# Attention heads in pairs of groups: shared transposes, and maxima found further ahead

## The chip, the cores and the metric

One core of a Trainium2 chip runs the whole program in one launch. The metric is the device time of one execution in microseconds, median of five runs. All arithmetic is in float32.

## What is computed

Two transformer-like blocks over an input of 8 batches, 512 tokens, 128 channels. The change lies in the attention of the first block:

```python
h = layernorm(x) * (1 + ca) + sa
Q, K, V = (lora_linear(h, ...).reshape(8, 512, 16, 8) for each)      # 16 heads of 8 channels
energy = einsum('nqhd,nkhd->nhqk', Q, K) / sqrt(8)
out = einsum('nhqk,nkhd->nqhd', softmax(energy), V).reshape(8, 512, 128)
x = x + ga * lora_linear(out, Wo, ...)
```

Behind it come a mixture of experts (top 2 of 8, and a shared one), and a second block with a state-space scan and another mixture of experts, whose last layer uses the weight `fut`.

## The kernel before

**Groups.** The 128 channels of a batch lie on 128 partitions, which form four strips of 32 rows. Each strip holds four heads of 8 channels. A *group* is one head out of each strip, so a batch has four groups and all batches have 32, g = 0 to 31; `m = g % 4` is the head's place in its strip. `split(g)` (on GpSimd) multiplies queries and keys by a mask that leaves only head m of each strip, as `qt` and `kt`, and sets one spare row of `kt` to 1. When the spare row of `qt` holds minus the largest score of a query, the product of `kt` and `qt` is already shifted for the softmax.

**Steps and slots.** A group takes four *steps* (one for each 128 keys or queries) and each step has two halves, each half two strips. A *slot* is one half step; the work runs through `slot(s)` for s below zero (a start-up) to 255 and a little beyond. Group g has its scores in slots 8g to 8g + 7, a batch has 32 slots. In one slot:

- `scores(t, half)` multiplies `kt` and `qt` of two strips (matmuls `ps`, line 535); `exps` takes the exponentials on ScalarE into tiles `es`.
- `maxima(u, 1 - half)` multiplies the other way round on the other two strips (matmuls `pm`, line 488), for a step u that is `LEAD` = 6 steps ahead, and VectorE reduces to the largest of each row, into a column of a pad `mpad`. There is one pad for each m.
- then whatever is registered for the slot in the dictionary `after`, in the order in which it was registered.

`after` holds, relative to the group: `split(g)` at 8g - 16; `max_done(g)` at 8g - 3, which transposes the pad (four matmuls `pmt`, line 523) and subtracts it from `qt` on VectorE; `weigh(g, qc)` at 8g + 9, 11, 12, 13, which multiplies `es` by the values (`av`, line 556, 16 matmuls into the four column strips of one bank) and copies the bank to `part` on ScalarE; and `normalise(g)` at 8g + 15, which transposes `part` (four matmuls `ppt`, line 574), takes reciprocals of the sums and multiplies on VectorE into `o`. The values stand in `vaug`, 32 columns for each head: 8 of values, one of ones, and the rest zero.

Relative to the batch b (slots 32b + ...): `load_stats` (VectorE) at -40 to -37, `load_root` (GpSimd) at -35, `load_batch` at -30 (normalised tokens `xh`, on GpSimd), -24 (transposes `ptn`) and +20 (adds a bias to x, GpSimd); `project_batch` at -18 and -17 (matmuls `pqk`, then `qf` and `kf` on ScalarE); `values` at +2; `channels_back` at 42 (`pot`), `out_proj` at 46 (`py`, added to x on VectorE; its weight `wo` comes from GpSimd), `out_stats` at 47 to 50. From 51 on come the tokens' normalisation, the router's transposes `ptf` and product `pl`, the choice of experts, the counts `pcount`, and eight indirect writes (scatters) on GpSimd. Every engine works strictly in the order of the program.

**Buffers.** PSUM has two pools here: four banks (`sc`) that `ps`, `av`, `pmt`, `ppt`, `py` and the like take in turn, and two pairs of banks (`mx`) that `pm` and `pqk` take in turn. A buffer is free again when the last reader of it is done.

**Constants.** `fut_sb`, the weight of the last layer, is zeroed on GpSimd at the very start and loaded by four of the early DMAs; its use is in `ff_weights`, near the end.

Of the kernel before, what the change touches and what calls it, by code (L numbers as in the profile page):

```python
# [23 lines left out]
HD = 8  # L24
# [44 lines left out]
def tile_adaln_two_blocks(  # L69
# [51 lines left out]
    l1w_sb = ct([P, 10, D], "l1w_sb")  # L121
    rb_sb = ct([P, NE], "rb_sb")
    fdt_sb = ct([P, 32], "fdt_sb")
    fut_sb = ct([P, NC4, D], "fut_sb")
    fdb_sb = ct([P, 1], "fdb_sb")

    def load_later():

        Q.dma_start(out=wrout_sb, in_=wrout)
        Q.dma_start(out=b2_sb[0:NE, :], in_=b2)  # L130
        c_bs2 = COLS["bs2"][0]
        Q.dma_start(out=b2_sb[NE : NE + 1, :], in_=pcols[:, c_bs2 : c_bs2 + 1].rearrange("p o -> o p"))
        Q.dma_start(out=ws1, in_=w1t[:, NE, :])
        Q.dma_start(out=ws2, in_=w2t[:, NE, :, :])
        Q.dma_start(out=win_sb, in_=win)
        Q.dma_start(out=ssm_sb, in_=ssm)
        Q.dma_start(out=l1w_sb, in_=l1w)
        Q.dma_start(out=rb_sb, in_=rb.partition_broadcast(P))
        Q.dma_start(out=fdt_sb, in_=fdt)

        for c in range(NC4):
            g = slice(32 * c, 32 * c + 32)
            Q.dma_start(out=fut_sb[g, c, :], in_=fut)
            Q.dma_start(out=fdb_sb[g, :], in_=fdb)

    def col(name, i=0, n=1):
# [30 lines left out]
    G.memset(fut_sb, 0.0)  # L177
    zeros = ct([P, P], "zeros")
    V.memset(zeros, 0.0)
    mpads = []  # L180
    for m in range(4):
        mp = ct([P, NC4, P], f"mpad{m}")
        G.memset(mp, 0.0)
        mpads.append(mp)
# [111 lines left out]
    with tc.tile_pool(name="at", bufs=2) as at, tc.tile_pool(name="sc", bufs=4, space=PSUM) as psc, tc.tile_pool(  # L296
# [5 lines left out]
        for i in range(2):  # L302
            va = ate.tile([P, NC4, 16, 32], FP, tag=f"vaug{i}", name=f"vaug{i}")
            G.memset(va, 0.0)
            G.memset(va[:, :, :, HD], 1.0)
            vaugs.append(va)

        def pair(name):
# [159 lines left out]

        def split(g):

            b, m = g // 4, g % 4
            sp = (m + 1) % 4
            qt = ate.tile([P, S], FP, tag="qt", name="qt", bufs=3)
            kt = ate.tile([P, S], FP, tag="kt", name="kt", bufs=3)
            (V if g == 0 else G).tensor_scalar(qt, batch[b]["q"], mask[:, m : m + 1], zero, ALU.mult, ALU.add)
            G.tensor_scalar(kt, batch[b]["k"], mask[:, m : m + 1], spare[:, sp : sp + 1], ALU.mult, ALU.add)
            group[g] = (qt, kt)

        def maxima(u, half):

            g, qc = u // 4, u % 4
            qt, kt = group[g]
            r0 = HD * ((g + 1) % 4)
            pm = pair("pm")
            for i in range(2):
                r = 32 * (2 * half + i)
                pin(
                    T.matmul(  # L488
                        pm[:, i, :],
                        lhsT=qt[r : r + 32, qc * P : (qc + 1) * P],  # L490
                        rhs=kt[r : r + 32, :],
                        start=True,
                        stop=True,
                    )
                )
            mp = mpads[g % 4][:, qc, :].rearrange("p (j r) -> p j r", r=32)
            return lambda: V.tensor_reduce(mp[:, 2 * half : 2 * half + 2, r0], pm, AX.X, ALU.max)

        def maxima_first(u):

            g, qc = u // 4, u % 4
            qt, kt = group[g]
            r0 = HD * ((g + 1) % 4)
# [9 lines left out]
            mp = mpads[g % 4][:, qc, :].rearrange("p (j r) -> p j r", r=32)  # L513
            V.tensor_reduce(mp[:, 0:2, r0], pm, AX.X, ALU.max)
            for j in (2, 3):
                V.tensor_reduce(mp[:, j : j + 1, r0], banks[j], AX.X, ALU.max)

        def max_done(g):

            qt, _ = group[g]  # L520
            pt = bank("pmt")
            for c in range(NC4):
                pin(T.transpose(pt[:, c, :], mpads[g % 4][:, c, :], ident))  # L523
# [24 lines left out]
        def weigh(g, qc):  # L548
# [4 lines left out]
            for kc in range(NC4):  # L553
                for j in range(4):
                    pin(
                        T.matmul(  # L556
                            ps[32 * j : 32 * j + 32, 0, :],
                            lhsT=vaugs[b % 2][:, kc, 4 * j + m, :],
                            rhs=es_of[4 * g + kc, j][:, q],
                            start=(kc == 0),  # L560
                            stop=(kc == NC4 - 1),
                        )
                    )
            if qc == 0:
                part_of[g] = at.tile([P, NC4, P], FP, tag="part", name="part")
            A.copy(part_of[g][:, qc, :], ps[:, 0, :])

        def normalise(g):
# [8 lines left out]
            p4 = pt.rearrange("p c (j r) -> p c j r", r=32)  # L577
            rd = stat.tile([P, NC4, 4], FP, tag="rd", name="rd")
            V.reciprocal(rd, p4[:, :, :, HD])
            o4 = batch[b]["o"].rearrange("p c (j m d) -> p c j m d", j=4, m=4)[:, :, :, m, :]  # L580
            V.tensor_tensor(o4, p4[:, :, :, 0:HD], rd.unsqueeze(3).to_broadcast([P, NC4, 4, HD]), ALU.mult)

        def channels_back(b):
            o = batch[b]["o"]
# [45 lines left out]
        for i, (src, dst) in enumerate(rows):  # L630
            at_slot(3 + i, lambda src=src, i=i: mod_rows(src, i))
            at_slot(8 + i, lambda dst=dst, i=i: mod_rows_in(dst, i))
        for b in range(B):
            for c in range(NC4):
                at_slot(32 * b - 40 + c, lambda b=b, c=c: load_stats(b, c))
            if b == 0:
                at_slot(-35, lambda: load_root(0, 0))
                at_slot(-32, lambda: load_root(0, 1))
            else:
                at_slot(32 * b - 35, lambda b=b: load_root(b))  # L640
            for i, s in enumerate((-30, 20, -24)):
                at_slot(32 * b + s, lambda b=b, i=i: load_batch(b, i))
            for i in range(2):
                at_slot(32 * b - 18 + i, lambda b=b, i=i: project_batch(b, i))
# [249 lines left out]
        for i in range(TABLE):  # L894
            at_slot(32 * PB[0] + (45, 47, 49, 59, 60, 62, 63)[i], lambda i=i: table(0, i))

        def slot(s):
            t, half_ = s // 2, s % 2
            u = t + LEAD
            if t < 0 <= u and half_ == 0:  # L900
                maxima_first(u)
# [270 lines left out]
        def pointwise():  # L1172
# [355 lines left out]
        def ff_weights(b):  # L1528
            f = ffn[b]
            f["up"] = ek.tile([P, NC4, D], FP, tag="futg", name="futg", bufs=3)  # L1530
            gate = mpads[b // 4][:, b % 4 : b % 4 + 1, :].to_broadcast([P, NC4, D])
            (V if b == last else G).tensor_tensor(f["up"], fut_sb, gate, ALU.mult)

        def ff_up(b):

# [272 lines left out]
```

## Time and profile before

| what | value |
|---|---|
| median of five runs | 1064.18 us (1061.27 to 1064.9) |
| profiled execution: its time, its span | 1061.22 us, 1059.5 us |
| mean granted TensorE clock | 0.976 |
| TensorE, weight loads, VectorE, ScalarE, GpSimd busy | 95%, 62%, 61%, 60%, 45% |
| attention's slots 0 to 255 | from 35.1 us to about 539 us |
| `pmt` and `ppt` transposes | 128 and 128 matmuls, 21.0 and 21.2 us busy |

PE is TensorE, DVE VectorE, ACT ScalarE, POOL GpSimd, SP the queue that issues most DMAs. A timeline line gives start, duration, engine, source line, operation, what it writes and reads, and the count of records; a float32 matmul leaves two records where its rows are 512 long and its operands 32 rows deep. What stands in square brackets is the idle time before it, and who ended it. In a group's line the two numbers after the first bar are busy microseconds and mean nanoseconds of one.

### The profile page before, as it was taken

To read this page: it belongs to the slowest core of one execution; us is meant where nothing else is said; L and a number is where in the kernel's file an instruction comes from. 1 tells how busy PE (TensorE), PEld (TensorE's weight loads), DVE (VectorE), ACT (ScalarE), POOL (GpSimd) and SP (SyncE) were. 2 spreads that over 40 slices of the span, in tenths; PEclk is the share of its full clock that TensorE was granted. 3 is DMA by queue.
4 is the path that set the end of the run, shared out by engine and by line. 5 is a ranking of instruction groups with operands and counts; after the bars stand their busy time and mean duration, and the time that the engine had idled before them with its cause. 6 is when DMAs were issued, how large, how long until landed. Compare 5 with 4: busy or idle time off the path is not lost.

```text
span 1059.5 us, 24424 instructions
## 1 busy us (share of the span) xinstructions
PE 1002.2 (95%) x9656; PEld 659.7 (62%) x9656; DVE 649.4 (61%) x1279; ACT 636.4 (60%) x1401; POOL 480.5 (45%) x756
## 2 busy tenths in 40 slices
PE   9999999999999999999989999949999988989897
PEld 7555555555555555555569999838787656556455
DVE  5967686777768777777621124115586648858663
ACT  1466676666767667676645666414587465686553
POOL 3313143554726546354373134355633348556652
PEclk9999999999999999999999999969899999999999
DMA  6199200000000000000227886611364024314051
GB/s 173 41 305 284 90 12 2 9 24 2 29 4 14 20 4 29 2 26 8 66 66 222 242 252 201 178 52 31 104 181 120 26 78 144 100 61 140 11 190 40
DMA packets 94914, 94.90 MB, mean 90 GB/s; under 512 B 7848, under 2 KB 72832, under 8 KB 94800
## 3 DMA queue, kind: packets, MB, share of 16 engines
q1 hardware_dynamic: 90528, 84.65, 26.7%
q0 software_dynamic: 4096, 8.40, 2.6%
q8 instruction: 76, 1.25, 0.5%
q14 instruction: 38, 0.31, 0.1%
q10 hardware_dynamic: 176, 0.30, 0.1%
HBM read 61.96 MB, written 31.36 MB: 88 GB/s over the span
## 4 chain that ended last, share of the span: by engine, by line
PE 79%; POOL 7%; DVE 6%; ACT 5%; issue 3%; DVEq 0%; POOLq 0%; ACTq 0%
PE ps L535 23%; PE av L556 12%; PE pyb L1048 10%; PE ph L1037 10%; PE pm L488 3%; PE r L1445 2%; PE pe L1457 2%; PE pmt L523 2%; POOL t L65 2%; PE ppt L574 2%; PE pqk L448 1%; DVE xc L65 1%; PE pyb L1007 1%; PE pw L1357 1%; PE pxt L962 1%
## 5 line engine op out<-in xcount | busy, mean ns | idle before, releaser
L65 DVE TENSOR_REDUCE mpad<-pm 128x2 f32<-128x1024 f32 (+1 forms) x262 | 310.4, 1194 | 110.2 <-PE pm L488 107.1
L65 ACT ACTIVATE es<-ps 128x512 f32<-128x512 f32 x512 | 275.6, 598 | 160.0 <-PE pm L488 135.8
L535 PE MATMUL ps<-qt,kt 32*128 32x512 f32 x1024 | 291.2, 630 | 0.7 <-DVE x L65 0.6
L488 PE MATMUL pm<-kt,qt 32*128 32x512 f32 x976 | 261.5, 636 | 0.0
L556 PEld LDWEIGHTS av<-es,vaug 128*32 128x32 f32 x4096 | 104.2, 109 | 94.1 <-ACT part L65 43.2
L556 PE MATMUL av<-es,vaug 128*32 128x128 f32 x4096 | 137.7, 276 | 0.0
L535 PEld LDWEIGHTS ps<-qt,kt 32*128 32x128 f32 x1024 | 93.9, 183 | 61.5 <-issue 30.8
L65 ACT ACTIVATE hid<-ph,bias 128x256 f32<-128x256 f32 x184 | 72.2, 477 | 52.1 <-PE ph L1037 50.2
L1048 PEld LDWEIGHTS pyb<-w2b,hid 128*128 128x128 f32 x736 | 89.8, 192 | 6.2 <-ACT hid L65 3.4
L790 POOL DMA_INDIRECT x_rows<-tok,ux x64 | 65.2, 1019 | 62.4 <-DMA x_rows<-tok,ux 55.9
L1048 PE MATMUL pyb<-w2b,hid 128*128 128x128 f32 x736 | 90.7, 276 | 2.6 <-ACT hid L65 2.6
L1037 PE MATMUL ph<-xt,w1b 128*128 128x256 f32 x368 | 90.0, 388 | 1.6 <-issue 1.6
L1068 POOL DMA_INDIRECT yg<-y_rows,yrows x64 | 65.0, 1016 | 37.2 <-PE pgt L1000 18.7
L488 PEld LDWEIGHTS pm<-kt,qt 32*128 32x128 f32 x976 | 73.1, 183 | 8.7 <-ACT kf L65 5.4
L1037 PEld LDWEIGHTS ph<-xt,w1b 128*128 128x128 f32 x368 | 67.8, 195 | 10.0 <-issue 2.3
L65 POOL TENSOR_SCALAR qt<-qf,mask,zero 128x512 f32<-128x512 f32 x31 | 23.9, 772 | 109.9 <-PE pm L488 93.0
L1457 PE MATMUL pe<-x,l1w_sb 128*128 128x512 f32 x128 | 67.6, 624 | 4.6 <-ACT ye L65 4.5
L65 DVE COPY xt<-pxt 128x256 f32<-128x256 f32 x46 | 19.2, 419 | 85.1 <-PE pxt L962 76.9
L1445 PEld LDWEIGHTS r<-l1w_sb,t 128*128 128x128 f32 x368 | 47.6, 196 | 27.0 <-POOL t L65 12.2
L65 ACT ACTIVATE ye<-pe,pc 128x512 f32<-128x512 f32 x64 | 42.9, 683 | 32.4 <-PE pe L1457 26.6
L1445 PE MATMUL r<-l1w_sb,t 128*128 128x128 f32 x368 | 50.4, 282 | 9.1 <-POOL t L65 7.4
L65 ACT ACTIVATE hid<-ph,pc 128x256 f32<-128x256 f32 x64 | 25.2, 479 | 35.7 <-remote 19.0
(304 smaller groups left out, 1552.3 us busy)
## 6 DMA issues: line engine op xcount, KB each, us to landing
x_rows<-zeros SPq DMA_DIRECT2D x16, 1024.0 KB
gb<-g_rows SPq DMA_DIRECT2D x32, 512.0 KB
w1b<-in_w1t SPq DMA_DIRECT2D x46, 256.0 KB
w2b<-in_w2t SPq DMA_DIRECT2D x46, 256.0 KB
xg<-x_rows SPq DMA_DIRECT2D x46, 128.0 KB
y_rows<-yb SPq DMA_DIRECT2D x46, 128.0 KB
x<-in_x SPq DMA_DIRECT2D x8, 256.0 KB
h_chan<-hf SPq DMA_DIRECT2D x8, 256.0 KB
```

The lines of the kernel that those rows point to most:

```text
L65: return lambda *args, **kwargs: self.pin(call(*args, **kwargs))
L488: T.matmul(pm[:, i, :], lhsT=qt[r : r + 32, qc * P : (qc + 1) * P], rhs=kt[r : r + 32, :], start=True, stop=True,)
L523: pin(T.transpose(pt[:, c, :], mpads[g % 4][:, c, :], ident))
L535: T.matmul(ps, lhsT=kt[r : r + 32, kc * P : (kc + 1) * P], rhs=qt[r : r + 32, :], start=True, stop=True)
L556: T.matmul(ps[32 * j : 32 * j + 32, 0, :], lhsT=vaugs[b % 2][:, kc, 4 * j + m, :], rhs=es_of[4 * g + kc, j][:, q], start=(kc == 0), stop=( ...
L574: pin(T.transpose(pt[:, c, :], part[:, c, :], ident))
L790: nc.gpsimd.indirect_dma_start(out=x_rows[h], out_offset=IndirectOffsetOnAxis(ap=chosen["ux", b][:, k, c : c + 1], axis=0), in_=half[h]["t ...
L1037: pin(T.matmul(ph[:, f, :], lhsT=it["w1"][:, f * P : (f + 1) * P], rhs=it["x"], start=True, stop=True))
L1048: T.matmul(py[:, c, :], lhsT=it["hid"][:, f, c * P : (c + 1) * P], rhs=it["w2"][:, f, :], start=(f == 0 and "shared" not in it), stop=(f = ...
L1068: nc.gpsimd.indirect_dma_start(out=gathered[b][:, k, c, :], out_offset=None, in_=y_rows[h], in_offset=IndirectOffsetOnAxis(ap=half[h]["yro ...
L1445: T.matmul(ffn[b]["r"][:, c, :], lhsT=x[:, c * P : (c + 1) * P], rhs=w, start=(start and c == 0), stop=stop, skip_group_check=True,)
L1457: pin(T.matmul(pe, lhsT=l1w_sb[:, 2 + e, :], rhs=x1s[b], start=True, stop=True))
```

## The change

Groups 2k and 2k + 1 become a pair. Both write their maxima into one pad, in different columns (the spare row moves from head m + 1 to m + 2 of the strip), so from group 6 on one set of transposes serves two groups: `max_done(g, 2)` at 8g - 3 for even g, with two updates of `qt`. Groups 0 to 5 keep a set each (`PAIRED` = 6). The values of odd heads stand 16 columns further right in `vaug`, so the results of a pair don't overlap: the even group's `weigh` copies to `part` on ScalarE as before, the odd group's adds to the same `part` on VectorE, and `normalise` serves both, at 8g + 23.

Maxima of both groups of a pair must be there before the first is used. They still begin six steps ahead; in each of the slots 13, 17, ... 41 (`TWICE`) a second half follows, so that they are ten steps ahead from slot 41 on, and end after slot 235 instead of 243. `split` moves to 8g - 24 with four buffers, and the loading of batch 1 comes two slots earlier, that of later batches eight slots earlier; `values` moves to -4. Two pads go, and `fut_sb` is zeroed (VectorE) and loaded in the second block.

```diff
-    for m in range(4):
+    for m in range(2):
         mp = ct([P, NC4, P], f"mpad{m}")
...
+    TWICE = range(13, 45, 4)
+    PAIRED = 6
...
-            A.copy(
-                vaugs[b % 2].rearrange("p c h r -> p (c h) r")[:, :, 0:HD],
-                flat(ps).rearrange("p (c d) -> p c d", d=HD),
-            )
+            for e in range(2):
+                A.copy(
+                    vaugs[b % 2].rearrange("p c (n e) r -> p (c n) e r", e=2)[:, :, e, 16 * e : 16 * e + HD],
+                    flat(ps).rearrange("p (n e d) -> p n e d", e=2, d=HD)[:, :, e, :],
+                )
...
-            sp = (m + 1) % 4
-            qt = ate.tile([P, S], FP, tag="qt", name="qt", bufs=3)
+            sp = (m + 2) % 4
+            qt = ate.tile([P, S], FP, tag="qt", name="qt", bufs=4)
...
-            mp = mpads[g % 4][:, qc, :].rearrange("p (j r) -> p j r", r=32)
+            mp = mpads[g // 2 % 2][:, qc, :].rearrange("p (j r) -> p j r", r=32)
...
-        def max_done(g):
+        def max_done(g, n):
             pt = bank("pmt")
             for c in range(NC4):
-                pin(T.transpose(pt[:, c, :], mpads[g % 4][:, c, :], ident))
-            V.scalar_tensor_tensor(qt, flat(pt), -1.0, qt, ALU.mult, ALU.add)
+                pin(T.transpose(pt[:, c, :], mpads[g // 2 % 2][:, c, :], ident))
+            for k in range(n):
+                qt, _ = group[g + k]
+                V.scalar_tensor_tensor(qt, flat(pt), -1.0, qt, ALU.mult, ALU.add)
...
+            if g % 2:
+                part = part_of[g - 1][:, qc, :]
+                V.tensor_tensor(part, part, ps[:, 0, :], ALU.add)
+                return
...
-            at_slot(8 * g - 16, lambda g=g: split(g))
-            at_slot(8 * g - 3, lambda g=g: max_done(g))
+            at_slot(8 * g - 24 if g > 4 else (-16, -8, 0, 8, 14)[g], lambda g=g: split(g))
+            if g < PAIRED:
+                at_slot(8 * g - 3, lambda g=g: max_done(g, 1))
+            if g % 2 == 0:
+                if g >= PAIRED:
+                    at_slot(8 * g - 3, lambda g=g: max_done(g, 2))
+                at_slot(8 * g + 23, lambda g=g: normalise(g))
...
-            at_slot(8 * g + 15, lambda g=g: normalise(g))
...
+            early_by = (0, 2)[b] if b < 2 else 8
+            t = 32 * b - early_by
...
-            at_slot(32 * b + 2, lambda b=b: values(b))
+            at_slot(32 * b - 4 if b else 2, lambda b=b: values(b))
...
+        to_find = iter([(u, h) for u in range(LEAD, STEPS) for h in (1, 0)])
...
-            reduce = maxima(u, 1 - half_) if 0 <= t and u < STEPS else None
+            reduce = [maxima(*u) for _, u in zip(range((s >= 0) + (s in TWICE)), to_find)]
             exps(t, found)
-            if reduce is not None:
-                reduce()
+            for do in reduce:
+                do()
...
+            fut_sb = k1["fut"] = lt([P, NC4, D], "fut_sb")
+            V.memset(fut_sb, 0.0)
+            for c in range(NC4):
+                Q.dma_start(out=fut_sb[32 * c : 32 * c + 32, c, :], in_=fut)
```

More of the change, by code (lines that the diff above doesn't have):

```diff
@@ L123, in tile_adaln_two_blocks @@
     fdt_sb = ct([P, 32], "fdt_sb")
-    fut_sb = ct([P, NC4, D], "fut_sb")
     fdb_sb = ct([P, 1], "fdb_sb")
@@ L142, in load_later @@
             g = slice(32 * c, 32 * c + 32)
-            Q.dma_start(out=fut_sb[g, c, :], in_=fut)
             Q.dma_start(out=fdb_sb[g, :], in_=fdb)
@@ L176, in tile_adaln_two_blocks @@
     V.memset(zero, 0.0)
-    G.memset(fut_sb, 0.0)
     zeros = ct([P, P], "zeros")
@@ L304, in tile_adaln_two_blocks @@
             G.memset(va, 0.0)
-            G.memset(va[:, :, :, HD], 1.0)
+            for e in range(2):
+                G.memset(va.rearrange("p c (n e) r -> p c n e r", e=2)[:, :, :, e, 16 * e + HD], 1.0)
             vaugs.append(va)
@@ L463, in values @@
                 )
-            A.copy(
-                vaugs[b % 2].rearrange("p c h r -> p (c h) r")[:, :, 0:HD],
-                flat(ps).rearrange("p (c d) -> p c d", d=HD),
-            )
+            for e in range(2):
+                A.copy(
+                    vaugs[b % 2].rearrange("p c (n e) r -> p (c n) e r", e=2)[:, :, e, 16 * e : 16 * e + HD],
+                    flat(ps).rearrange("p (n e d) -> p n e d", e=2, d=HD)[:, :, e, :],
+                )
         def split(g):
             b, m = g // 4, g % 4
-            sp = (m + 1) % 4
-            qt = ate.tile([P, S], FP, tag="qt", name="qt", bufs=3)
-            kt = ate.tile([P, S], FP, tag="kt", name="kt", bufs=3)
+            sp = (m + 2) % 4
+            qt = ate.tile([P, S], FP, tag="qt", name="qt", bufs=4)
+            kt = ate.tile([P, S], FP, tag="kt", name="kt", bufs=4)
             (V if g == 0 else G).tensor_scalar(qt, batch[b]["q"], mask[:, m : m + 1], zero, ALU.mult, ALU.add)
@@ L482, in maxima @@
             qt, kt = group[g]
-            r0 = HD * ((g + 1) % 4)
+            r0 = HD * ((g + 2) % 4)
             pm = pair("pm")
@@ L502, in maxima_first @@
             qt, kt = group[g]
-            r0 = HD * ((g + 1) % 4)
+            r0 = HD * ((g + 2) % 4)
             pm = pair("pm")
@@ L512, in maxima_first @@
                 )
-            mp = mpads[g % 4][:, qc, :].rearrange("p (j r) -> p j r", r=32)
+            mp = mpads[g // 2 % 2][:, qc, :].rearrange("p (j r) -> p j r", r=32)
             V.tensor_reduce(mp[:, 0:2, r0], pm, AX.X, ALU.max)
@@ L516, in maxima_first @@
                 V.tensor_reduce(mp[:, j : j + 1, r0], banks[j], AX.X, ALU.max)
-        def max_done(g):
-            qt, _ = group[g]
+        def max_done(g, n):
             pt = bank("pmt")
             for c in range(NC4):
-                pin(T.transpose(pt[:, c, :], mpads[g % 4][:, c, :], ident))
-            V.scalar_tensor_tensor(qt, flat(pt), -1.0, qt, ALU.mult, ALU.add)
+                pin(T.transpose(pt[:, c, :], mpads[g // 2 % 2][:, c, :], ident))
+            for k in range(n):
+                qt, _ = group[g + k]
+                V.scalar_tensor_tensor(qt, flat(pt), -1.0, qt, ALU.mult, ALU.add)
         def scores(t, half):
@@ L576, in normalise @@
                 batch[b]["o"] = at.tile([P, NC4, D], FP, tag="o", name="o", bufs=1)
-            p4 = pt.rearrange("p c (j r) -> p c j r", r=32)
-            rd = stat.tile([P, NC4, 4], FP, tag="rd", name="rd")
+            p4 = pt.rearrange("p c (j e r) -> p (c j) e r", j=4, e=2)
+            rd = stat.tile([P, NC4 * 4, 2], FP, tag="rd", name="rd")
             V.reciprocal(rd, p4[:, :, :, HD])
-            o4 = batch[b]["o"].rearrange("p c (j m d) -> p c j m d", j=4, m=4)[:, :, :, m, :]
-            V.tensor_tensor(o4, p4[:, :, :, 0:HD], rd.unsqueeze(3).to_broadcast([P, NC4, 4, HD]), ALU.mult)
+            o4 = batch[b]["o"].rearrange("p c (j m d) -> p (c j) m d", j=4, m=4)[:, :, m : m + 2, :]
+            V.tensor_tensor(o4, p4[:, :, :, 0:HD], rd.unsqueeze(3).to_broadcast([P, NC4 * 4, 2, HD]), ALU.mult)
         def channels_back(b):
@@ L633, in tile_adaln_two_blocks @@
         for b in range(B):
+            early_by = (0, 2)[b] if b < 2 else 8
+            t = 32 * b - early_by
             for c in range(NC4):
-                at_slot(32 * b - 40 + c, lambda b=b, c=c: load_stats(b, c))
+                at_slot(t - 40 + c, lambda b=b, c=c: load_stats(b, c))
             if b == 0:
@@ L639, in tile_adaln_two_blocks @@
             else:
-                at_slot(32 * b - 35, lambda b=b: load_root(b))
-            for i, s in enumerate((-30, 20, -24)):
-                at_slot(32 * b + s, lambda b=b, i=i: load_batch(b, i))
+                at_slot(t - 35, lambda b=b: load_root(b))
+            for i, s in enumerate((t - 30, 32 * b + 20, t - 24)):
+                at_slot(s, lambda b=b, i=i: load_batch(b, i))
             for i in range(2):
-                at_slot(32 * b - 18 + i, lambda b=b, i=i: project_batch(b, i))
-            at_slot(32 * b + 2, lambda b=b: values(b))
+                at_slot(t - 18 + i, lambda b=b, i=i: project_batch(b, i))
+            at_slot(32 * b - 4 if b else 2, lambda b=b: values(b))
             at_slot(32 * b + 42, lambda b=b: channels_back(b))
@@ L895, in tile_adaln_two_blocks @@
             at_slot(32 * PB[0] + (45, 47, 49, 59, 60, 62, 63)[i], lambda i=i: table(0, i))
+        to_find = iter([(u, h) for u in range(LEAD, STEPS) for h in (1, 0)])
         def slot(s):
             t, half_ = s // 2, s % 2
-            u = t + LEAD
-            if t < 0 <= u and half_ == 0:
-                maxima_first(u)
+            if t < 0 <= t + LEAD and half_ == 0:
+                maxima_first(t + LEAD)
             found = scores(t, half_) if 0 <= t < STEPS else []
-            reduce = maxima(u, 1 - half_) if 0 <= t and u < STEPS else None
+            reduce = [maxima(*u) for _, u in zip(range((s >= 0) + (s in TWICE)), to_find)]
             exps(t, found)
-            if reduce is not None:
-                reduce()
+            for do in reduce:
+                do()
             for do in after.get(s, []):
@@ L1531, in ff_weights @@
             gate = mpads[b // 4][:, b % 4 : b % 4 + 1, :].to_broadcast([P, NC4, D])
-            (V if b == last else G).tensor_tensor(f["up"], fut_sb, gate, ALU.mult)
+            (V if b == last else G).tensor_tensor(f["up"], k1["fut"], gate, ALU.mult)
         def ff_up(b):
```

## The prediction

> **What bounds the kernel now.** I read the page first (busy time, groups), then the order of the matmuls in steady attention, then the three places where that order breaks. Attention lasts to 544.6 us; the 515 us behind it are not touched but for one weight. The page:
>
> ```profile
> PE 1002.2 (95%) x9656; PEld 659.7 (62%) x9656; DVE 649.4 (61%) x1279; ACT 636.4 (60%) x1401; POOL 480.5 (45%) x756
> ...
> L65 DVE TENSOR_REDUCE mpad<-pm 128x2 f32<-128x1024 f32 (+1 forms) x262 | 310.4, 1194 | 110.2 <-PE pm L488 107.1
> ```
>
> TensorE is full, VectorE has 39% to spare, and its main work is one reduction of 1.19 us for each half step. The timeline of TensorE in the second batch:
>
> ```profile
> 103.82 0.70 PE L535 MATMUL ps<-qt,kt 32*128 32x512 f32 x2
> 103.84 0.70 PE L488 MATMUL pm<-kt,qt 32*128 32x512 f32 x2
> 104.36 0.59 PE L535 MATMUL ps<-qt,kt 32*128 32x512 f32 x2
> 104.37 0.59 PE L488 MATMUL pm<-kt,qt 32*128 32x512 f32 x2
> 104.89 1.08 PE L556 MATMUL av<-es,vaug 128*32 128x128 f32 x32
> 105.91 0.66 PE L523 MATMUL pmt<-ident,mpad 128*128 128x128 f32 x4
> 106.49 0.70 PE L535 MATMUL ps<-qt,kt 32*128 32x512 f32 x2
> ```
>
> Scores (ps) use two of four 32-row strips and the maxima (pm) the other two, so both together take 1.07 us (103.82 to 104.89), one `weigh` 1.02, four transposes 0.58. Taking these and the projections' own rows, a batch of 32 slots adds up to 61.8 us; the trace has 63.83, the same in four batches running. So TensorE sets the end, and about 2 us a batch are waits. The same view later, where VectorE ran late and then had no maxima left:
>
> ```profile
> 513.02 1.13 PE L535 MATMUL ps<-qt,kt 32*128 32x512 f32 x4
> 513.90 1.13 PE L488 MATMUL pm<-kt,qt 32*128 32x512 f32 x4
> 514.87 1.02 PE L535 MATMUL ps<-qt,kt 32*128 32x512 f32 x4
> 515.43 1.13 PE L488 MATMUL pm<-kt,qt 32*128 32x512 f32 x4
> 516.49 1.08 PE L556 MATMUL av<-es,vaug 128*32 128x128 f32 x32
> 517.50 1.13 PE L535 MATMUL ps<-qt,kt 32*128 32x512 f32 x4
> 518.56 1.08 PE L556 MATMUL av<-es,vaug 128*32 128x128 f32 x32
> ```
>
> Scores alone cost 1.06 (517.50 to 518.56): beside scores the maxima are free. Out of step they cost a round of their own, 0.97 (513.90 to 514.87).
>
> **Transposes removed.** `max_done` runs 19 times instead of 32, `normalise` 16 instead of 32: 29 sets of four. By spacing a set takes 0.585 (105.91 to 106.49, and 0.59 for ppt): 29 x 0.585 = 17.0 us, all on the path. The group's busy time (21.0 us for 128) would make it 19.0, but that counts overlap; I take 17.0. *The Trainium skill, TensorEngine Tiling (Array Packing), Key Properties, says that a change of tiling mode drains TensorE; no row here separates such a drain. By the 0.11 us from one transpose's start to the next a set would be 0.44 and the sum 12.8; the spacing of 0.585 holds whatever a change of mode adds.*
>
> **The eight doubled slots** (13, 17, ... 41). The order of halves is (1, 0), one per slot; an extra one turns it, so in slots 14 to 16, 22 to 24, 30 to 32 and 38 to 40 maxima fall on the strips of the scores, and in the doubled slots one of the two does. Bounds from the rows: at best the eight extra halves cost 8 x 0.97 = 7.8; at worst they and the twelve turned slots, 20 x 0.97 = 19.4. Walking slots 13 to 17 with the rows' durations from the start of 13 (reduction 1.2, two pm bank pairs): the projection pqk of batch 1, now at slot 12, holds one pair, so the second half waits for the first's reduction and starts at 2.5; `weigh` ends at 4.6; `max_done` of group 2 reads the pad that groups 2 and 3 now share, so its transposes wait for the second reduction and end at 5.5. The maxima of 14 follow its scores on the same strips and end at 7.6; then VectorE works without a break to 13.6, the last pm waits for a bank until 11.2, and `weigh` ends at 13.3. Before, these slots are 2.67 + 3 x 1.06 + 2.08 = 7.9: +5.4, less 1.1 that the same projection costs before two slots later (128.46, below). So +4.3; slots 21 to 25 (no shared pad in use, but ppt between) 12.7 against 9.0, +3.7; 29 to 33 (shared pad, ptn) +3.0; 37 to 41 (pqk inside) +3.9. Sum +14.9, nearer to the upper end since VectorE's 1.19 exceeds the 0.97 to 1.06 of TensorE. *The Trainium skill, same page, PSUM Bottleneck, warns that tiling speeds TensorE but not the emptying of PSUM, which speaks against two halves in a slot. It gives no price.*
>
> **Steady batches.** In odd groups `weigh` ends in a VectorE add (no row; nearest o<-ppt,rd, 0.29, and ScalarE's copy 0.27): 64 x 0.27 = 17 us more on VectorE, 75% to about 80% of this stage; ScalarE loses as much. Behind the add stand statistics and the next reduction, and the bank goes back later. Two `qt` updates in a row (2 x 0.69) hold the pmt bank until 4.15 after slot 13 of a batch begins; `load_stats` moves from slots 24 to 27 onto 16 to 19, beside `out_stats`. Walked through slots 13 to 23, waits add up to 1.0 instead of 1.2, but pqk, now at slot 6 instead of 14, loses VectorE the slack it gave and leaves its own wait there:
>
> ```profile
> 128.45 0.49 PEld L488 LDWEIGHTS pm<-kt,qt 32*128 32x128 f32 x8 [0.77 <-ACT kf L65]
> ```
>
> I take +0.3 for six batches, +1.8. GpSimd's queue: `load_root` (2.5) and xh (3.15) now stand ahead of the `tok` products among the scatters; two scatter waits of 1.5 swallow 3.0 of it, and ptf had 3.9 us of slack (341.98 to 345.84), so about 1 remains: +0.2. Together +2.0; between -1 (all hidden) and +8 (one lone pm round, 0.97, in each batch more, and 0.5 at ptf).
>
> **Start.** Slot -3 transposes pad 0 after group 1's first maxima went into it: the transposes wait for three reductions (30.12 to about 32.8), and scores begin near 37 instead of 35.14: +1.9; statistics that come two slots earlier fill VectorE's idle time there (0.6), and GpSimd's three memsets less give 0.1. +1.2, 0 to 2.5.
>
> **End.** Maxima stop at slot 235 instead of 243, so VectorE is free while it makes batch 6's statistics, on which GpSimd waits before the last scatters, the tables and `wo`:
>
> ```profile
> 518.83 0.24 POOL L65 TENSOR_SCALAR var<-mv_l0f 128x4 f32<-128x4 f32 x1 [7.38 <-DVE mv_l0f L65]
> ...
> 549.51 0.45 POOL L65 TENSOR_TENSOR wo<-wqk,ga_rows 128x128 f32<-128x128 f32 x1
> ```
>
> TensorE waits for that `wo` 1.91 us. The queue starts about 3.65 sooner by the same walk; 1.75 of it are three transpose sets counted above, so -1.9. TensorE alone would gain more (the lone rounds at 513, a late part copy of 1.1), but GpSimd then ends last; 0 to -3.5.
>
> **At nothing:** the two half copies of `values` (0.2 more on ScalarE, idle 40%), the wider `normalise` (VectorE, half as many), and `fut_sb` later: a memset on VectorE (under 0.6) and four issues of 0.42 on SP, with block weights asked for two to four blocks of 4 us ahead; uncovered, 2 us.
>
> **Sum:** -17.0 + 14.9 + 2.0 + 1.2 - 1.9 = -0.8, on a profiled execution of 1061.2 (span 1059.5), which lies 3.0 below the median of 1064.18. So 1063.4; the case's own range is 1060 to 1067. About 0.2% (2.1 us) is what a measurement here can tell from no change.
>
> **Rivals.** *A, the advance is cheap:* the doubled slots cost little over 7.8 because neighbouring slots' halves overlap strip against strip; then 6 us less, 1057. For it: at 522.23 scores of two slots start together. Against it: VectorE's rate. *B, VectorE becomes late in every batch:* the place is slots 13 to 23, where double `qt` update, residual add, two sets of statistics and the adds meet; once the lag exceeds the slack of one `weigh` slot (2.08 - 1.19 - 0.29 = 0.6), each batch pays two lone rounds, 6 x 2 x 0.97 less the 1.8 counted, so 9.8 - 0.8 = +9: 1073. For it: before, VectorE lag already makes 0.5 of waits at slot 24. Against it: it is busy 75% on average. *C, the transposes were only cover:* in three short slots (1.06 each) ScalarE's two exponentials (1.08 per slot) catch up under ppt or pmt; then half of the 17.0 returns as waits on score banks, 8.5 - 0.8 = +7.7: 1072. Against it: ScalarE is two thirds busy in this stage.
>
> **Numbers.** Forecast case 0.38 (0.10 faster, 0.22 same, 0.06 slower), A 0.30, B 0.26, C 0.06: faster 0.40, same 0.22, slower 0.38. The range 1055 to 1073 takes in most of A and half of B, and leaves out under 2 in 10.
>
> **What would show it.** pmt at 76 and ppt at 64 matmuls; a steady batch near 62; slots 13 to 17 about 13 us with reductions back to back; in a slot like 14 pm starting when ps ends. Batches of 61.5 and doubled groups of 10 us mean A; batches above 63 with pm waiting on mpad in slots 16 to 21 mean B; ps waiting on es at slots 6 to 9 means C. If GpSimd's statistics still wait to 16.7 us after slot 237 begins, the end step is wrong.

## Result and the profile after

The changed kernel takes 1066.49 us (median of 27 runs, 1060.74 to 1069.44) beside 1063.69 for the kernel before (52 runs): ratio 1.0024, 95% interval 1.0015 to 1.0034. It is slower by 0.15 to 0.34%; the forecast was no change, 1063.4. Its profiled execution took 1064.66 us with a span of 1062.9. The page, TensorE, VectorE and the reductions:

```profile
PE 1001.2 (94%) x9540; PEld 658.4 (62%) x9540; DVE 658.0 (62%) x1312; ACT 618.3 (58%) x1345; POOL 477.3 (45%) x755
...
L65 DVE TENSOR_REDUCE mpad<-pm 128x2 f32<-128x1024 f32 (+1 forms) x262 | 308.9, 1195 | 105.5 <-PE pm L493 95.5
```

The 116 transposes are gone (pmt 76 matmuls, ppt 64), the reductions are as many and as long as before, yet TensorE is busy only 1.0 us less: some of the work that is left takes longer. The timeline of TensorE in slot 13, the first doubled one:

```profile
62.71 0.70 PE L542 MATMUL ps<-qt,kt 32*128 32x512 f32 x2
62.72 0.70 PE L493 MATMUL pm<-kt,qt 32*128 32x512 f32 x2
...
65.25 1.13 PE L493 MATMUL pm<-kt,qt 32*128 32x512 f32 x4 [1.40 <-DVE mpad L65]
66.31 1.45 PE L563 MATMUL av<-es,vaug 128*32 128x128 f32 x32
67.69 1.12 PE L528 MATMUL pmt<-ident,mpad 128*128 128x128 f32 x4
68.73 1.91 PE L542 MATMUL ps<-qt,kt 32*128 32x512 f32 x7
```

The second half waits 1.40 us for the first's reduction, as foreseen. Not foreseen is what comes after: `weigh` takes 1.45 instead of 1.08 and four transposes 1.04 by spacing instead of 0.585. The windows view (last three columns: granted clock, DMA share, GB/s) says why, here and at the start, where the transposes of slot -3 waited for the next group's reductions on the shared pad:

```profile
32.05 0.66 PE L528 MATMUL pmt<-ident,mpad 128*128 128x128 f32 x4 [1.80 <-DVE mpad L65]
```

```profile
32.00:36.00 4.00, 3.96 (x22) 2.87 (x22) 0.69 (x1) 0.00 (x0) 4.00 (x6) 0.59 0.00 0
...
64.00:68.00 4.00, 2.75 (x38) 1.61 (x39) 2.42 (x2) 1.15 (x4) 0.37 (x1) 0.86 1.04 311
68.00:72.00 4.00, 4.00 (x23) 2.34 (x22) 1.17 (x2) 2.01 (x5) 1.10 (x2) 0.71 0.98 285
```

After each of these waits the granted clock fell, to 0.59, and to 0.86 and 0.71; in the same windows of the kernel before it was 1.00. The wait for kf stands where the prediction put it, now in slot 8 and again in every batch (weight loads of TensorE):

```profile
379.62 0.30 PEld L493 LDWEIGHTS pm<-kt,qt 32*128 32x128 f32 x4 [0.77 <-ACT kf L65]
```

At the end of attention GpSimd's queue moved forward, as foreseen (the last column in brackets was 7.38 before):

```profile
523.09 0.23 POOL L65 TENSOR_SCALAR var<-mv_l0f 128x4 f32<-128x4 f32 x1 [2.98 <-DVE mv_l0f L65]
...
553.93 0.45 POOL L65 TENSOR_TENSOR wo<-wqk,ga_rows 128x128 f32<-128x128 f32 x1
```

Slot by slot (a slot starts with its first score), the two profiled executions differ like this; "behind it" ends with VectorE's last computing instruction, 3.2 us ahead of the span's end in both. One projection of 1.9 us, which the change moves across slot 45, is counted where it was:

| stretch | before, us | after, us | difference | the prediction's sum |
|---|---|---|---|---|
| start to slot 0 | 35.14 | 37.74 | +2.6 | +1.2 |
| slots 0 to 45 | 83.83 | 101.95 - 1.9 | +16.2 | +14.9 less two ppt sets, +13.7 |
| slots 45 to 237 | 383.11 | 371.01 + 1.9 | -10.2 | 24 sets, -14.0, and +2.0: -12.0 |
| slot 237 to last py of attention | 47.94 | 43.74 | -4.2 | three sets, -1.75, and -1.9: -3.65 |
| behind it | 506.2 | 505.2 | -1.0 | 0 |
| sum | | | +3.4 | -0.8 |

So the saving came and was eaten: by the start, the doubled slots and the steady batches, 1.4, 2.5 and 1.8 us more than forecast. Of the 1.8, some 0.3 to 0.7 belong to this one execution: in the six later profiles with the same steady batch, slots 45 to 237 take 370.3 to 370.7 us instead of 371.0.

### The profile page after: what moved, and what is told of

It is laid out like the page before. It is cut to its first block, busy times and chain, and to the rows that moved or that the text cites. A ratio compares the mean times of both kernels' runs of the same rounds, so it can differ in the third digit from the quotient of the medians.

```text
span 1062.9 us, 24186 instructions
## 1 busy us (share of the span) xinstructions
PE 1001.2 (94%) x9540; PEld 658.4 (62%) x9540; DVE 658.0 (62%) x1312; ACT 618.3 (58%) x1345; POOL 477.3 (45%) x755
## 3 DMA queue, kind: packets, MB, share of 16 engines
q8 instruction: 75, 1.23, 0.5%
## 4 chain that ended last, share of the span: by engine, by line
PE 77%; DVE 7%; POOL 6%; ACT 5%; issue 3%; DMA 1%; DVEq 0%; POOLq 0%; ACTq 0%
PE ps L542 21%; PE av L563 11%; PE pyb L1066 10%; PE ph L1055 9%; PE pm L493 5%; PE r L1467 2%; PE pe L1479 2%; POOL t L65 2%; DVE mpad L65 1%; PE pqk L451 1%; DVE xc L65 1%; PE pmt L528 1%; PE pyb L1025 1%; PE pw L1379 1%; PE pxt L980 1%
## 5 line engine op out<-in xcount | busy, mean ns | idle before, releaser
L65 DVE TENSOR_REDUCE mpad<-pm 128x2 f32<-128x1024 f32 (+1 forms) x262 | 308.9, 1195 | 105.5 <-PE pm L493 95.5
L65 ACT ACTIVATE es<-ps 128x512 f32<-128x512 f32 x512 | 273.6, 600 | 171.5 <-PE pm L493 116.0
L542 PEld LDWEIGHTS ps<-qt,kt 32*128 32x128 f32 x1024 | 99.8, 184 | 71.8 <-issue 28.2
L65 ACT ACTIVATE hid<-ph,bias 128x256 f32<-128x256 f32 x184 | 72.0, 475 | 52.6 <-PE ph L1055 49.1
L493 PEld LDWEIGHTS pm<-kt,qt 32*128 32x128 f32 x976 | 77.0, 183 | 21.3 <-DVE mpad L65 8.9
L65 POOL TENSOR_SCALAR qt<-qf,mask,zero 128x512 f32<-128x512 f32 x31 | 23.8, 767 | 122.8 <-PE pm L493 58.3
L65 DVE COPY xt<-pxt 128x256 f32<-128x256 f32 x46 | 19.2, 419 | 85.0 <-PE pxt L980 73.7
L65 ACT ACTIVATE ye<-pe,pc 128x512 f32<-128x512 f32 x64 | 42.8, 682 | 32.5 <-PE pe L1479 26.7
L1066 PE MATMUL pyb<-ws,hid 128*128 128x128 f32 x256 | 38.1, 300 | 10.6 <-issue 10.5
```

The costliest lines, as they stand in the source:

```text
L65: return lambda *args, **kwargs: self.pin(call(*args, **kwargs))
L493: T.matmul(pm[:, i, :], lhsT=qt[r : r + 32, qc * P : (qc + 1) * P], rhs=kt[r : r + 32, :], start=True, stop=True,)
L542: T.matmul(ps, lhsT=kt[r : r + 32, kc * P : (kc + 1) * P], rhs=qt[r : r + 32, :], start=True, stop=True)
L1066: T.matmul(py[:, c, :], lhsT=it["hid"][:, f, c * P : (c + 1) * P], rhs=it["w2"][:, f, :], start=(f == 0 and "shared" not in it), stop=(f = ...
```

## Experiments

They ran on four chips on which the kernel before takes 1039.0 to 1040.5 us instead of 1063.7; each ratio is against runs of the kernel before on the same chip. The changed kernel itself was not timed there. Attention can be compared across chips, as the unchanged kernel showed:

> The kernel before, unchanged, for its profile on this chip. The runs with pairs alone and with other doubled slots took 1038 to 1044 us beside 1039.5 for the kernel before on their chip, against 1063.7 where the change was first measured; their profiles differ from the first ones behind 690 us, where TensorE's granted clock was 0.5 for 20 us in the first ones. Theory (the stage behind attention differs by granted clock alone, attention does not): batches of 63.8 us, slot 45 to 237 in 383.1 us to within 0.5 us, whatever the total. Rival (the chip is faster in attention too): batches shorter by over 0.3 us.

Measured: 1042.21 us; batches of 63.83, and slots 45 to 237 within 0.01 us of the first profile. Behind attention it took 488.8 us from the first ph to VectorE's last instruction where the first chip took 510.0. Most of that lies in waits of TensorE that the waits view of the first chip's kernels, before and after, puts down to "issue" (total, times, longest), and that do not appear on the other chip:

```profile
PE ph L1037 <- issue: 10.1, 8, 2.2
```

```profile
PE pyb L1066 <- issue: 10.5, 9, 1.7
```

In the same stretch of the first chip's profile before, from 694.85 to 718.74 us, the granted clock was 0.50. What held TensorE up there is not shown.

The start, too, moved: the first score of the unchanged kernel came at 37.40 instead of 35.14, with the same instructions.

**What the eight doubled slots cost.** Two theories: VectorE's rate, which the prediction named, or the strips. One run shortened VectorE's part:

> The changed kernel, doubled slots at 13, 17, ... 41 as they are, but the reduction of each extra half reads 64 of its 512 columns, so that its maximum is that of 64 keys only (it leaves out the rest). VectorE is spared about 8 x 1.0 us, TensorE's matmuls and their order stay. If VectorE's rate sets the price of the doubled slots: slots 12 to 45 take 72 to 76 us instead of 80.97. If the strips on TensorE do: 79 to 81. If each has a share, between.

```diff
-            reduce = [maxima(*u) for _, u in zip(...)]
+            reduce = [maxima(*u, (S, 64)[i]) for i, u in zip(...)]   # second half of a slot: 64 columns
```

Measured: slots 12 to 45 in 80.05 us instead of 80.97 (ratio 1.0040, 1.0016 to 1.0063). The extra reductions took 0.29 us instead of 1.23; 7.5 us less work on VectorE bought 0.9. VectorE's rate is not the price. Two runs moved the extra halves:

> The changed kernel with the eight doubled slots at 17, 20, 25, 28, 33, 36, 41, 44 instead of 13, 17, ... 41. The order of halves stays (1, 0), so each odd one still turns the strips for three slots; but these now hold two slots with a weigh in each group of three, where before they were the short slots 6, 7 and 0 of a group. From the start of slot 12 to that of slot 45 the changed kernel takes 80.97 us, the one before 63.04. Theory (VectorE's rate of 1.19 us a reduction sets the price of the doubled slots, as in the walk of the prediction): weigh gives VectorE time, and the stretch falls to 71 to 75. Rival (the strips set it: scores and maxima on the same strips one after the other): twelve turned slots as before, so 79 to 81, less about 1 for slot 13, where a projection holds a pair of banks.

> As the kernel with the other doubled slots (17, 20, 25, ... 44), but the order of halves goes by strip: each slot takes the next half of the two strips that its scores leave free, and a doubled slot takes one more half of the other two. So no slot is turned, and only the eight extra halves themselves stand alone. If turned strips are a large part of the price, the stretch from slot 12 to 45 is 3 to 6 us shorter than in the kernel that has the same doubled slots in the order (1, 0): at 0.97 for each extra half 63.04 - 4.7 (eight pmt and ppt sets less in it) + 7.8 = 66 to 70. If VectorE alone sets it, the two kernels differ by under 1.5 us.

```diff
-    TWICE = range(13, 45, 4)
+    TWICE = (17, 20, 25, 28, 33, 36, 41, 44)          # both runs
...
-        to_find = iter([(u, h) for u in range(LEAD, STEPS) for h in (1, 0)])
+        left_of = [iter(range(LEAD, STEPS)), iter(range(LEAD, STEPS))]   # by strip only
...
-            reduce = [maxima(*u) for _, u in zip(range((s >= 0) + (s in TWICE)), to_find)]
+            strips = [1 - half_, half_][: (s >= 0) + (s in TWICE)]
+            reduce = [maxima(u, h) for h in strips for u in [next(left_of[h], None)] if u is not None]
```

Measured, slots 12 to 45: 77.96 with the other slots (ratio 1.0035, 1.0017 to 1.0053), 73.66 by strip (0.9994, 0.9972 to 1.0016). The first is just below the 78 to 80 of the strips and well above VectorE's 71 to 75: place is worth 3.0 us, slot 13's wait and the clock after it among them. The same slots by strip are worth 4.3 more, as the strip theory asked. That 73.66 is above its 66 to 70 comes from the expectation's own sum: in these slots two sets of transposes are missing, not eight, and batch 2's projection of 1.9 us has moved in. With these, 73.66 - 63.04 + 1.17 - 1.9 leaves 9.9 us for the eight extra halves, 1.2 each. TensorE's timeline of a turned slot with the other slots in the order (1, 0):

```profile
76.93 1.13 PE L542 MATMUL ps<-qt,kt 32*128 32x512 f32 x4
77.89 1.30 PE L493 MATMUL pm<-kt,qt 32*128 32x512 f32 x8
```

Scores first, then maxima, one behind the other. By strip, in the doubled slot 20:

```profile
75.85 0.70 PE L542 MATMUL ps<-qt,kt 32*128 32x512 f32 x2
75.87 0.70 PE L493 MATMUL pm<-kt,qt 32*128 32x512 f32 x2
...
76.40 1.71 PE L493 MATMUL pm<-kt,qt 32*128 32x512 f32 x6
78.04 1.08 PE L563 MATMUL av<-es,vaug 128*32 128x128 f32 x32
```

Scores and the regular half start together; only the extra half stands alone. The slot lasts 2.19 up to `weigh` instead of 1.06, so the extra half costs 1.13, and no slot behind it is turned.

**What the shared pad costs.**

> The changed kernel with a third pad: while max_done still serves one group (groups 0 to 5), odd groups write their maxima into a pad of their own, wiped by two GpSimd memsets between groups, so that a max_done no longer waits for the next group's first reductions. In the changed kernel the transposes of slot -3 wait 1.80 us and the granted clock is 0.59 in the 4 us after that; slots 13 to 18 take 14.62. Theory (the shared pad makes the late start, the wait itself and the clock after it): first score at 35.0 to 35.8 instead of 37.7, slots 13 to 18 and 29 to 34 shorter by 0.5 to 1.5 together, 2.5 to 4 us in all. Rival (the start is late by chance of the clock: the kernel with pairs alone began at 37.39 with no such wait): start within 0.8 of 37.7, under 1.5 us in all.

```diff
-    for m in range(2):
+    for m in range(3):                                 # pads
...
+        def pad_of(g):                                 # the pad of a group, wherever one is named
+            return 2 if g < PAIRED and g % 2 else g // 2 % 2
...
+            if g in (1, 3):
+                at_slot(8 * g, lambda g=g: wipe(g))    # GpSimd clears the old group's columns
```

Measured: slots 13 to 18 in 13.03 instead of 14.62, slots 29 to 34 0.4 shorter; slot 255 begins at 536.82 instead of 541.45. The first score came at 36.09, between theory and rival. Its time varies by chance too. From 4 to 8 us TensorE works on 26 to 31 matmul records in ten of the profiles and on 19 in six, as here in two of the kernel before:

```profile
4.00:8.00 4.00, 4.00 (x29) 3.70 (x28) 2.40 (x11) 0.22 (x1) 3.89 (x7) 1.00 1.00 307
```

```profile
4.00:8.00 4.00, 4.00 (x19) 3.55 (x17) 3.88 (x13) 0.10 (x1) 3.56 (x6) 1.00 1.07 323
```

After the quick start the first score comes at 35.1 in the kernel before, at 37.5 to 38.1 with the shared pad (five profiles) and at 34.9 to 36.3 with the third pad (four); after the slow one at 37.4 without a shared pad (two), at 39.8 to 39.9 with it (three) and at 36.6 with the third (one). So chance moves the start by some 2.3 us, and like for like the shared pad costs 2.4 to 3.0: the late start of the changed kernel is not chance. The total stayed above that of the kernel before, at 1042.86 (ratio 1.0035, 1.0016 to 1.0054), which led to what follows attention, below. The same wait of 1.40 us stands in slot 13, and this time the clock stayed:

```profile
63.44 1.13 PE L496 MATMUL pm<-kt,qt 32*128 32x512 f32 x4 [1.40 <-DVE mpad L65]
64.50 1.08 PE L571 MATMUL av<-es,vaug 128*32 128x128 f32 x32
65.51 0.66 PE L531 MATMUL pmt<-ident,mpad 128*128 128x128 f32 x4
```

```profile
64.00:68.00 4.00, 4.00 (x56) 2.32 (x53) 1.92 (x2) 1.60 (x4) 0.77 (x1) 1.00 1.13 338
68.00:72.00 4.00, 3.80 (x24) 1.23 (x21) 3.77 (x4) 3.38 (x7) 2.75 (x3) 1.00 0.97 289
```

**What takes back the transposes in a steady batch.**

> The kernel before with the change's second half alone: odd groups' sums are added to the even group's part on VectorE and one normalise serves two groups. No early maxima, no shared max_done, no doubled slot, loading where it was. It saves 16 sets of ppt: 16 x 0.585 = 9.4 us. Theory (the transposes are worth their spacing, and what ate the rest is the advance of the maxima): about -9.4 plus at most 0.3 a batch for VectorE's adds and the wider normalise, so -7 to -9.5 against the kernel before, with steady batches of 62.7 to 63.0 instead of 63.83. Rival (the transposes were cover, or the adds make VectorE late in every batch): -3 or less, steady batches of 63.4 and more.

```diff
+            if g % 2:
+                part = part_of[g - 1][:, qc, :]
+                V.tensor_tensor(part, part, ps[:, 0, :], ALU.add)
+                return
...
-            at_slot(8 * g + 15, lambda g=g: normalise(g))
+            if g % 2 == 0:
+                at_slot(8 * g + 23, lambda g=g: normalise(g))
```

Measured: 1038.46 us, ratio 0.9991 (0.9972 to 1.0009); batch 63.77 instead of 63.83. The rival holds: sixteen sets of transposes, 9.4 us, were worth next to nothing alone. Per slot: 15 and 31 are 0.68 shorter each; 16 is 0.68 longer, 19, 25 and 9 are 0.19, 0.27 and 0.32 longer. Slot 16 in the timeline, and the same wait over the span in the waits view:

```profile
319.70 1.02 PE L537 MATMUL ps<-qt,kt 32*128 32x512 f32 x4
321.60 1.16 PE L490 MATMUL pm<-kt,qt 32*128 32x512 f32 x8 [0.87 <-ACT kf L65]
```

```profile
PE pm L490 <- ACT kf L65: 6.2, 7, 0.9
```

In the kernel before, the waits view has no such line for TensorE's matmuls, only one for their weight loads:

```profile
PEld pm L488 <- ACT kf L65: 5.4, 7, 0.8
```

Whether ppt stands in slot 15 or not, kf starts on ScalarE 6.37 us after slot 14 does (312.84 to 319.21 before, 314.48 to 320.85 here), and the maxima of slot 16 start when it gives the bank pair back. The other half of the loss lies in slots 19, 25 and 9, where VectorE's new work stands:

> The changed kernel with the 64 adds of the odd groups' sums left out: ScalarE copies them to a scratch tile that nothing reads, so the odd groups' part of the attention is missing. TensorE's work is the same. Theory (VectorE's adds of 0.28 take back part of the transposes in each batch, as the run with pairs alone suggests, where slots 19, 25 and 9 grew by 0.78 together): batch 61.4 to 61.8 instead of 62.19. Rival (the adds are hidden, as the prediction had it to 0.3 a batch): 62.0 to 62.2.

```diff
-                V.tensor_tensor(part, part, ps[:, 0, :], ALU.add)
+                A.copy(idle_part, ps[:, 0, :])             # and ones at both places of every head in vaug
```

Measured: batch 61.93, all 0.26 of it in slots 19 and 24. That lies between the two expectations and is what the prediction had put on the adds (0.3). Slot 25 keeps its 2.46, so that part belongs to the wider normalise.

> The changed kernel with the projection of q and k for batches 2 to 7 at slots 3 and 4 of the batch before instead of 6 and 7. At 6 it falls on three short slots, and the maxima of slot 8 wait 1.1 us for the bank pair that the copy kf gives back. In the run with pairs alone the removal of ppt from slot 15 was taken back to the hundredth by this same wait (slot 15 0.68 shorter, slot 16 0.68 longer). Theory (transposes and waits on kf are one cover for the other): batch 62.19 to 61.0 - 61.5, 5 to 7 us in all. Rival (VectorE or ScalarE is the bound of that stretch and another wait takes its place): batch 61.9 or more, under 2 us in all.

```diff
-                at_slot(t - 18 + i, lambda b=b, i=i: project_batch(b, i))
+                at_slot((t - 18 if b < 2 else 32 * b - 29) + i, lambda b=b, i=i: project_batch(b, i))
```

Measured: batch 62.50, ratio 1.0067 (1.0042 to 1.0091). The theory fell: the wait moved with the projection (slot 5 is 0.78 longer, slot 9 0.62).

> As the kernel with strips, third pad and fut_sb late, and besides the copies kf and qf both right behind the projection in its slot, kf first; so the bank pair does not wait for the exponentials of a slot more. In the changed kernel the maxima of slot 8 wait 1.1 us a batch for kf. Theory (ScalarE's order behind the projection makes that wait): batches 0.4 to 1.1 us shorter, 3 to 7 us in all. Rival (ScalarE is what lags in the short slots 6 to 8, so that the exponentials now come late instead): under 0.2 a batch, or longer.

```diff
...
+                d["k"] = ate.tile([P, S], FP, tag="kf", name="kf", bufs=2)
+                A.activation(d["k"], ps[:, 1, :], AF.Identity, bias=col("bk"))
                 d["q"] = ate.tile([P, S], FP, tag="qf", name="qf", bufs=2)
...
-                d["k"] = ate.tile([P, S], FP, tag="kf", name="kf", bufs=2)      # where they stood, a slot later
-                A.activation(d["k"], d.pop("ps")[:, 1, :], AF.Identity, bias=col("bk"))
```

Measured: 1029.45 us, ratio 0.9911 (0.9889 to 0.9933); batch 61.93, 0.26 shorter. Slot 8 gives 0.95, slot 9 takes 0.70 of it back, where loads for the scores now wait for the exponentials (`[0.39 <-ACT es L65]`), as the rival has it. So ScalarE's order makes part of the wait, and its lag in the short slots lies beneath. Less came than the theory hoped.

> The changed kernel with each normalise two slots later (slots 9 and 25 of a batch instead of 7 and 23), behind a weigh and ahead of one short slot, where VectorE has had 2.08 us for one reduction. With the adds on ScalarE a batch went from 62.19 to 61.93, all of it in slots 19 and 24; slot 25 kept 2.46 against 2.19 before. Theory (the wider normalise, 0.35 + 0.42 us on VectorE instead of 0.25 + 0.29, makes the next reductions late in the short slots): slot 25 back at 2.2, slot 0 unchanged, batch 61.7 to 62.0. Rival (any normalise there costs the same transposes and the same lag, wherever it stands): batch 62.1 or more.

```diff
-                at_slot(8 * g + 23, lambda g=g: normalise(g))
+                at_slot(8 * g + 25, lambda g=g: normalise(g))
```

Measured: batch 62.85, 0.66 longer. Slot 25 is 2.87, but it now holds the set of ppt, 0.68; without it 2.19 remain, so its lag of 0.27 is gone, as the theory said. But slot 7 lost its ppt (1.66 to 0.98), and slot 8 grew from 2.18 to 2.86: the wait on kf came out from under it, as a new line of TensorE's matmuls in the waits view. (Slot 9, with ppt, is 0.59 longer; slot 10, 0.46, which is not explained.)

```profile
PE pm L493 <- ACT kf L65: 5.3, 6, 0.9
```

**What lies behind attention.** By strip, attention ended 5.5 us ahead of the unchanged kernel (533.3 against 538.8 at slot 255), and the total was the same. The run that was to add the parts came out likewise:

> Order of halves by strip with doubled slots 17, 20, ... 44, the third pad, and the projection at slots 3 and 4, all three in the changed kernel. If they add: attention (first score of slot 255) at 533.3 - 2.5 to 4 - 5 to 7 = 523 to 526, against 541.5 in the changed kernel and 536.6 before. The total should then be 8 to 14 us below the kernel before. Rival (what attention saves is paid back by the granted clock behind it, as the run by strip suggests with attention at 533.3 and the same total as before): within 4 us of the kernel before.

Measured: 1039.80, ratio 1.0002 (0.9985 to 1.0020), slot 255 at 533.81. Most of the gain was gone behind attention. SP's queue in the kernel with the third pad, and GpSimd's first gather there and in the kernel before on the same chip:

```profile
663.19 3.03 SPq L65 DMA_DIRECT2D fut_sb<-in_fut  x4
```

```profile
680.13 0.98 POOL L1096 DMA_INDIRECT yg<-y_rows,yrows  x1 [20.57 <-DMA hl<-h_chan]
```

```profile
679.63 0.98 POOL L1068 DMA_INDIRECT yg<-y_rows,yrows  x1 [17.46 <-DMA hl<-h_chan]
```

The four loads of fut_sb hold SP for 3.03 us ahead of hl, and the gather waits for hl 3.1 us longer, though the first ph came 2.6 us sooner.

> The changed kernel with the memset of fut_sb and its four loads at step 58 of the second stage instead of 28. At step 28 the four issues hold SP's queue for 2.9 to 3.0 us ahead of xg, y_rows and hl, and GpSimd's first yg then comes 3.1 us later against TensorE (134.3 instead of 131.3 us behind the first ph, third pad against the kernel before on the same chip); ptn of the next stage follows. The prediction put this at nothing, 2 us if uncovered. Theory (the four issues cost 2 to 4 us where no other stall covers them): 2 to 4 us less than the changed kernel, about 1040 to 1041 beside 1039 of the kernel before, first yg back at 131 behind the first ph. Rival (the stage differs by the clock alone): within 1 us of the changed kernel on this chip (1043 to 1044), first yg as late as before.

```diff
         when(28, pointwise)                            # without the memset and the four loads
+        when(58, fut_in)                               # which stand here
```

Measured: first yg 131.1 us behind the first ph (134.3 with the third pad), the stage from ph to the end 485.0 us; ratio 1.0021 (1.0004 to 1.0039). With the loads at step 28 that stage took 490.3 to 492.5 in seven runs and 485.0 in one; at step 58, 482.5 to 486.7 in four. On each of the four chips the profiles with the loads at step 28 are the longer ones there, by 1.7 to 8.0 us. The granted clock also varies there, so the exact share of the loads stays open; a total of 1042.10 is less of a gain than the theory asked for.

> Order of halves by strip with doubled slots 17, 20, ... 44, the third pad, and fut_sb at step 58, in the changed kernel; the projection where the change put it. If the parts add: first score of slot 255 near 532 (533.8 in the run that had the first two but the projection at slots 3 and 4, less 0.3 for each of six batches), 7 us ahead of the kernel before on this chip (538.8), the stage behind it as short as before, so 1030 to 1033 against 1039. Rival (what attention saves is paid back behind it by the clock or GpSimd's chain): 1036 or more.

Measured: 1031.94 us, ratio 0.9938 (0.9915 to 0.9961); slot 255 at 531.3, slots 12 to 45 in 72.90. The parts add, and this beats the kernel before on its chip. With the copies at once (above) it is 0.9911; and with the late normalise, harmful alone:

> The kernel with strips, third pad, fut_sb late and both copies at once, and each normalise two slots later. If the late normalise takes away a wait of its own: batch 61.5 to 61.8 instead of 61.93 and 1 to 2.5 us less than the run without it, so 1027 to 1029 beside 1039 of the kernel before. Rival: 1029 to 1031, as without it.

Measured: 1022.73 us, ratio 0.9843 (0.9819 to 0.9867). Batch 61.40, 0.53 shorter than without it: with kf early there is little left under slot 7's ppt (slot 8 takes 1.41 instead of 1.22). By slot 255 it is 0.9 us ahead of the run without it (2.3 counted from each run's own first score); the rest of the difference to 1029.45, on another chip, lies mostly behind attention (482.5 us from the first ph instead of 486.7), where the clock differs from run to run, and is not explained by the edit. These versions were not run on the chip where the change was first measured.

## Why the prediction was wrong

**Transposes: right in number and spacing, wrong in "all on the path".** 29 sets went, and TensorE's spacing did not change. In a steady batch of the changed kernel slots 5 and 21 are 0.59 us shorter and slots 15 and 31 0.68, but of these 2.5 us the batch keeps 1.64; and the pairs alone gave next to none of 9.4 us. A set is worth its 0.585 only where nothing waits beneath it. The prediction made this a rival (C, 0.06) and looked for the wait on the exponentials; it sat on kf, which the prediction itself had shown in a PEld line and priced only as VectorE's loss of slack.

**Doubled slots: failed in reason, and mis-sized.** The term was +14.9; in the table's cut +16.2 came for +13.7. Slots 0 to 18 lie 1.5 above the walk and 26 to 37 1.1, the others within 0.4. In slots 13 to 18 (14.62, the walk had 13.3) the granted clock fell after the 1.40 wait; with clock 1.00 and the third pad they take 13.03. Its ground, VectorE's 1.19 against TensorE's 1.06, did not hold: VectorE freed of three quarters of each extra reduction (0.29 us instead of 1.23) left 80.05 of 80.97. The price is strips and place: 3.0 us for the place, 4.3 for the turned strips, and about 9.9 for the extra halves themselves. The Trainium skill's warning about emptying PSUM (TensorEngine Tiling (Array Packing), PSUM Bottleneck), which the prediction weighed, points at VectorE; the runs do not bear it out here. Rival A, that halves overlap strip against strip, named the right lever, but only another order of halves pulls it.

**Steady batches: the step "at nothing" failed.** +2.0 was predicted and +3.8 came, 0.64 a batch. The adds cost 0.26, as sized. The wider normalise, put at nothing because there is half as much of it, ends slot 25 0.27 us later: one step of 0.77 us on VectorE in the short slots is worse than two of 0.54 apart. Slot 0 is 0.32 longer besides (2.12 to 2.44), which no run took apart. These three come to 0.85; other slots give some of it back. B did not happen: no batch reached 63, and in slots 16 to 21 of a steady batch no pm waits on mpad.

**Start: failed by half.** +1.2 was predicted and +2.6 came, between two executions with the same quick start. The wait of 1.80 was foreseen, the late start taken at 1.9 less 0.7; the clock of 0.5 after the wait was not foreseen, nor that the start of one and the same kernel varies by 2.3 us.

**End: right.** GpSimd's statistics wait to 12.4 us after slot 237 instead of 16.7, and the stretch to py is 4.2 shorter for 3.65.

**fut_sb: named, and luck on the first chip.** Uncovered, the prediction said, it costs 2 us. On the first chip the gather came 2.1 us later too (134.05 instead of 131.99 us behind the first ph), but the time behind attention did not grow; the "issue" waits of 10 us and more stand in the same stage there, and whether they hid the loads is not shown. On the other chips the stage was longer with the loads at step 28.

## What to carry to other kernels

Before counting a removed instruction as gain, look for what waits beneath it at that place: here a copy's bank, which the waits view listed only under the weight loads while the transposes hid it from the matmuls. Two edits that were worth -0.26 and +0.66 us a batch alone made -0.79 together. When work on different strips runs side by side, fix the order by strip, not by step: one extra half out of turn spoils every slot until the next. And put nothing on a DMA queue "for later" without reading who issues next on it.

## What the hardware showed

A short wait of TensorE may be paid twice, and whether it is hangs on its moment. The same wait of 1.9 us for `wo`, ahead of attention's last `py`, stands in fourteen of the sixteen profiles; in nine the granted clock was 0.5 for the next 3.41 us, in five it stayed at 1.00. In each trace the clock changes only on a raster of 3.41 us. In the nine, 1.89 us or more of the wait lie in one step of this raster; in the five a step ends within it, and no step holds more than 1.48. The wait of 1.80 in slot -3 was followed by 0.5 in all eight profiles that have it. That of 1.40 in slot 13 was in six of seven, where it lies in one step; in the seventh, with the third pad, a step ends at 62.96, within the wait from 62.04 to 63.44. This is worked out from the traces; no run moved a wait on purpose, and no threshold comes out of it (1.40 in slot 13 brought the drop, 1.48 ahead of `py` did not).

The Trainium skill, TensorE: Matmul & The Clock Gate, HAM oscillation, gives the rule as no idle gaps over about 3.4 us, and Part 1 says that its window runs free of the kernel's start; the second agrees with drops that hang on where a wait falls, the first is too generous for these runs.

The stage behind attention differed by 21 us between chips, with TensorE waiting for "issue" on one of them alone.
